# A graph attention layer on one core: gathers that wait for TensorE, and the output made behind the edge loop, in place of output made inside it and gathers that wait for their buffers alone

## The chip, the cores and the metric

One core of a Trainium2 chip runs the kernel. The metric is device time of one execution in microseconds (us). The engines are named as the profile names them: PE is TensorE (PEld its weight loads), DVE VectorE, ACT ScalarE, POOL GpSimd, SP SyncE. GpSimd's indirect DMAs fetch rows of a table by an index in memory ("gathers"); SyncE issues nearly all other transfers.

## What is computed

A graph has N = 12500 nodes with 128 features x, and E = 212500 edges, sorted by destination, with 128 features each, a weight, a source src and a destination dst. Reference, cut to what matters:

```python
h = relu(layernorm(x))
q = (h @ Wq.T + bq)            # 8 heads of 16
k = edge_attr @ Wk.T + bk      # one row per edge
v = (h @ Wv.T + bv)
in_m, out_m, diag_m = sum(q[src]*k), sum(q[dst]*k), sum(q[src]*q[dst])   # per edge and head
score = (seg_softmax(in_m/4, dst) + seg_softmax(out_m/4, dst) + seg_softmax(diag_m/4, dst)) * weight ** lam
g = segment_sum(score * v[dst], dst)
out = x + leaky_relu(g @ Wo.T + bo, 0.1)
```

Since v[dst] is the same for all edges of a destination, it is enough to sum exponentials (den) and weighted exponentials (num) per destination, three kinds by 8 heads each; the score of a node is num / den, and the rest is work per node.

## The kernel before

`ordered_path` holds all of it (a second path in the file is for inputs of another shape and isn't run here).

*First stage* (lines 645 to 920): the nodes are loaded, normalized and turned, q is made and stored as a table in DRAM (`q_table`), and once more as three bf16 terms (`q3_table`). Indices are laid out by blocks. The gathers of the first blocks start here.

*Edge loop* (lines 1233 to 1276). The edges are 416 blocks of 512, taken as S = 5 parts of the sorted list side by side, so that one *turn of t* (T = 84 of them) takes one block of each part: block number g = 5 t + s. A block's work:

- `gather` (621): four indirect DMAs on GpSimd, each 128 rows of `q_table` by src (line 625), into a buffer `qq`. There are QQ = 11 buffers, and turn g issues the gathers of block g + LOOK = g + 9. So they wait until block g - 2 has been read (line 1092 and 1093).
- `fetch_edges` (610): 512 rows of edge features, by SyncE, six blocks ahead.
- `turn` (1061): four PE transposes of the edge features, copied to SBUF by ScalarE as `eT`; `project` (1070): k of the block by PE (a bias matmul, line 1072, and the products, line 1074); `spread_q` (1079): q of the destinations by a matmul with one-hots (line 1083), copied beside the gathered rows by ScalarE (line 1085). `one_hots` (1053) makes the one-hots of the next t on ScalarE.
- `logits` (1087): VectorE multiplies (1092, 1093) and reduces (1095).

Once in five blocks, for the block row t - 1 or t - 2: `turn_logits`, `scan_max`, `powers`, `scan_sums` (VectorE's scans along 512 edges), `turn_sums`, `select`, `to_rows` (matmuls of line 1186, copied by ScalarE to `rows` in line 1191) and `put_rows`, in which SyncE stores five pieces of 42 nodes to DRAM, each part to a table of its own (`sums[s]`).

The order on each engine is the order of the program's calls: `pin` (592) chains an engine's instructions. Turn g of the loop calls, in this order,

```python
gather(g + LOOK); fetch_edges(g + AHEAD)
project(g + 1)
turn(g + 2); spread_q(g + 2)
logits(g)
one_hots(t + 1, s)
# by s: turn_logits, turn_sums | scan_max | to_rows, powers | scan_sums, fetch | select, put_rows
nodes_between(t, s)
```

so PE's *turn g* is k of block g + 1, transposes and one-hot products of block g + 2, and what stands there by s.

*Output.* A unit is 256 nodes; there are 49. The class `Nodes` (935) makes the output of two of them: `load_sums`, `load_x`, `normalize`, `scores`, `turn`, `project_v`, `turn`, `project_o`, `store`. 40 of the 49 units lie in one part only and are done before the last turns; `stored_at` (527) works out from when, and `nodes_between` (1206) makes two of them in each two turns of t, in pieces after the blocks' own work. The other 9 units come behind the loop (1279 to 1298). In the loop's first five turns ScalarE's queue zeroes the five tables of sums (1274).

Of the kernel before, what the change touches and what calls it, by code (L numbers as in the profile page):

```python
# [472 lines left out]
def ordered_path(ctx: ExitStack, tc: tile.TileContext, flag, x, src, dst, edge_attr, edge_weight,  # L473
# [17 lines left out]


# [22 lines left out]
    UN = 2 * P  # L515
    LAST = N // 2 - (NU - 1) * P
    assert NI % 2 == 0 and NU % CU == 0 and N % 2 == 0 and 96 <= LAST < P

    START, RATE, NEAR = round(G * BE * N / E), BE * N // E, 90

    def parts_of(u):

        return [s for s in range(S)
                if (s == 0 or START * s + RATE - NEAR < UN * (u + 1))
                and (s == S - 1 or UN * u < START * (s + 1) + RATE + NEAR)]

    def stored_at(u):

        of = parts_of(u)
        t = -(-(UN * (u + 1) + NEAR - START * of[0]) // RATE)  # L530
        return t + 2 if len(of) == 1 and t < T else None
# [6 lines left out]
    sums = [dram.tile([NP, 2 * H3], F32, name=f"sums{i}") for i in range(S)]  # L538
# [40 lines left out]
    blank = consts.tile([P, 2 * 2 * H3], F32, name="blank")  # L579
# [3 lines left out]
    bases = consts.tile([1, T, S], I32, name="bases")  # L583
    tops = consts.tile([1, T, S], I32, name="tops")
# [23 lines left out]
    qqs, st, eas = {}, {}, {}  # L608
# [12 lines left out]
    def gather(g):  # L621
        if g < S * T:
            qq = gath.tile([P, JN, 2, F], F32, name="qq")
            for j in range(JN):
                pin(nc.gpsimd.indirect_dma_start(  # L625
                    out=qq[:, j, 0, :], out_offset=None, in_=q_table,
                    in_offset=bass.IndirectOffsetOnAxis(
                        ap=src_i[:, g % S * G + g // S, j:j + 1], axis=0)))
            qqs[g] = qq
# [15 lines left out]
    with tc.tile_pool(name="prep", bufs=1) as prep, \  # L645
# [15 lines left out]
        for i, b in enumerate((bv, bk, bo)):  # L661
            pin(nc.sync.dma_start(b_row[:, i, :], b[None, :]))
        due = prep.tile([1, T, S], F32, name="due")
        nc.gpsimd.iota(due, pattern=[[RATE, T], [START, S]], base=0, channel_multiplier=0,
                       allow_small_or_imprecise_dtypes=True)
# [207 lines left out]
        for g in range(-2, GN):  # L873
            if g + 2 < GN:
                rectify(g + 2)
            if 0 <= g + 1 < GN:
                turn_h(g + 1)
            if g >= 0:
                nodes_q(g)
            ready(g + 4)  # L880
            measure(g + 6 + min(max(g, 0), 6))
            if g in side:
                side[g]()
# [10 lines left out]
        found = prep.tile([1, 7], F32, name="found")  # L894
# [4 lines left out]
        base_f = prep.tile([1, T, S], F32, name="base_f", tag="terms")  # L899
# [11 lines left out]
        nc.vector.tensor_reduce(found[:, 3:4], halo[:, 0:S - 2], AX.X, ALU.max)  # L911

        far = top_f
        nc.vector.tensor_sub(far, base_f, due)
        nc.vector.tensor_reduce(found[:, 4:5], far, AX.XY, ALU.min)
        nc.vector.tensor_scalar(found[:, 4:5], found[:, 4:5], -float(NEAR), None, op0=ALU.is_lt)
        nc.vector.tensor_reduce(found[:, 5:6], far[:, 0:2], AX.XY, ALU.max)
        nc.vector.tensor_scalar(found[:, 5:6], found[:, 5:6], float(NEAR), None, op0=ALU.is_gt)
        nc.vector.tensor_reduce(found[:, 6:7], found[:, 0:6], AX.X, ALU.max)
        nc.vector.tensor_copy(flag, found[:, 6:7])  # L920


    fin = ctx.enter_context(tc.tile_pool(name="fin", bufs=2))

    def unit_in(to, u):

        to = to.rearrange("p k f -> p (k f)")
        if u < NU - 1:
            pin(nc.sync.dma_start(to, units(x, u, 1, F)[:, 0, :]))
        else:  # L930
            pin(nc.gpsimd.memset(to[96:, :], 0.0))
            pin(nc.sync.dma_start(to[:LAST, :],
                                  x[u * UN:, :].rearrange("(p k) f -> p (k f)", k=2)))

    class Nodes:

        def __init__(self, of):
            self.of = of  # L940
            self.n = 2 * len(of)

        def load_x(self):
            self.x = fin.tile([P, JN, F], F32, name="x_in", bufs=4)
            for i, u in enumerate(self.of):
                unit_in(self.x[:, 2 * i:2 * i + 2, :], u)

        def load_sums(self):
            self.ab = fin.tile([P, JN, 2 * H3], F32, name="ab", bufs=3)
            for i, u in enumerate(self.of):  # L950
                for j, t in enumerate(parts_of(u)):
                    to = self.ab
                    if j > 0:
                        to = self.more = fin.tile([P, JN, 2 * H3], F32, name="more", bufs=3)
                    pin(nc.sync.dma_start(to[:, 2 * i:2 * i + 2, :].rearrange("p k c -> p (k c)"),
                                          units(sums[t], u, 1, 2 * H3)[:, 0, :]))
                    if j > 0:
                        both = self.ab[:, 2 * i:2 * i + 2, :]
                        pin(nc.vector.tensor_add(both, both, to[:, 2 * i:2 * i + 2, :]))

        def normalize(self, lo, hi):
            if lo == 0:
                self.h = fin.tile([P, JN, F], F32, name="h", bufs=4)
            for b in range(lo, min(hi, self.n)):
                n = 2 * self.of[b // 2] + b % 2
                pin(nc.scalar.activation(self.h[:, b, :], self.x[:, b, :], AF.Relu,
                                         bias=shift[:, n:n + 1], scale=inv[:, n:n + 1]))

        def scores(self):
            n = self.n  # L970
            den, num = self.ab[:, :n, 0:H3], self.ab[:, :n, H3:]
            pin(nc.vector.tensor_scalar(den, den, 1e-30, None, op0=ALU.max))
            pin(nc.vector.reciprocal(den, den))
            pin(nc.vector.tensor_mul(num, num, den))
            score = self.score = fin.tile([P, JN, HEADS], F32, name="score")
            pin(nc.vector.tensor_add(score[:, :n], num[:, :, 0:HEADS], num[:, :, HEADS:2 * HEADS]))
            pin(nc.vector.tensor_add(score[:, :n], score[:, :n], num[:, :, 2 * HEADS:]))

        def turn(self, to):
            for b in range(self.n):  # L980
                pin(nc.tensor.transpose(to[:, b, :], self.h[:, b, :], ident))
            self.hT = fin.tile([P, JN, P], F32, name="hT")
            pin(nc.scalar.copy(self.hT[:, :self.n], to[:, :self.n]))

        def product(self, to, bias, w):
            pin(nc.tensor.matmul(to[:, :self.n, :], ones3, bias[:, :self.n, :], start=True, stop=False))
            for b in range(self.n):
                pin(nc.tensor.matmul(to[:, b, :], self.hT[:, b, :], w, start=False,
                                     stop=(b == self.n - 1)))

        def project_v(self, to):
            self.product(to, bv3, wv)
            pin(nc.vector.tensor_mul(
                self.h[:, :self.n, :].rearrange("p n (h d) -> p (n h) d", d=DIM),
                to[:, :self.n, :].rearrange("p n (h d) -> p (n h) d", d=DIM),
                self.score[:, :self.n, :].rearrange("p n h -> p (n h)")[:, :, None]
                .to_broadcast([P, self.n * HEADS, DIM])))

        def project_o(self, to):
            n = self.n  # L1000
            self.product(to, bo3, wo)
            o, y = self.h[:, :n], self.x[:, :n]
            pin(nc.scalar.copy(o, to[:, :n]))
            pin(nc.vector.scalar_tensor_tensor(o, o, SLOPE, o, op0=ALU.mult, op1=ALU.max))
            pin(nc.vector.tensor_add(y, o, y))  # L1005

        def store(self):
            for i, u in enumerate(self.of):
                y = self.x[:, 2 * i:2 * i + 2, :].rearrange("p k f -> p (k f)")
                if u < NU - 1:  # L1010
                    pin(nc.sync.dma_start(units(out, u, 1, F)[:, 0, :], y))
                else:
                    pin(nc.sync.dma_start(out[u * UN:, :].rearrange("(p k) f -> p (k f)", k=2),
                                          y[:LAST, :]))


    pairs, todo = {}, sorted((stored_at(u), u) for u in range(NU) if stored_at(u) is not None)
    for t in range(0, T - 1, 2):
        if len(todo) > 1 and todo[1][0] <= t:
            pairs[t] = Nodes([todo.pop(0)[1], todo.pop(0)[1]])  # L1020
# [3 lines left out]
    with tc.tile_pool(name="work", bufs=2) as work, \  # L1024
# [181 lines left out]
        def nodes_between(t, s):  # L1206
            new, old = pairs.get(t - t % 2), pairs.get(t - t % 2 - 2)
            even = t % 2 == 0
            if new and even and s == 0:
                new.load_sums()  # L1210
                new.load_x()
# [3 lines left out]
            if new and even and s == 3:  # L1215
                new.normalize(2, 4)
# [127 lines left out]
```

## Time and profile before

| | us |
|---|---|
| three executions, lowest, median, highest | 3223.39, 3225.73, 3229.08 |
| the profiled execution | 3225.73 |
| its span, first to last instruction | 3223.6 |
| first stage, until the first reduction of the loop (line 1095) | 0 to 177.1 |
| edge loop, first to last reduction | 177.1 to 3149.5 |
| last gather's end | 3089.0 |
| behind the last reduction | 3149.5 to 3223.6 |
| gathers (line 625): 1680 | 1013 ns each in the mean, 0.30 between two |
| granted TensorE clock, mean | 0.713 |

The profile's rows are groups of instructions: line, engine, operation, output<-input tile and shape, count, busy time and mean duration of one, then the idle time of that engine just before them and what ended it. A row of the waits names who waited, for whom, the total, the count and the longest. "remote" there is a release whose origin the profile can't name; "issue" is idle time in which nothing that the profile shows was waited for.

### The profile page before, as it was taken

Reading aid. Unit: us, or ns where it says so; the run is one execution under the profiler, and the core shown is the slowest. Engines: PE = TensorE matmul, PEld = TensorE weight load, DVE = VectorE, ACT = ScalarE, POOL = GpSimd, SP = SyncE. Lnnn points to the kernel's source line nnn. Section 1 sums busy time; section 2 is a strip of 40 time slices with the busy share of each in tenths; the row PEclk is TensorE's granted clock in tenths of the full one; section 3 lists DMA queues with packets and bytes.
Section 4 is the critical chain, followed back from the end, with each engine's and each line's share of the span. In section 5 each row is a group of like instructions: output and inputs, shape, how many; then the busy total and the mean of one; then the engine's idle time right before and its main releaser. Section 6 shows DMA issues by size and latency. Waiting matters only on the chain. (4 is left out here: it accounts for less than half of the span.)

```text
span 3223.6 us, 35159 instructions
## 1 busy us (share of the span) xinstructions
PE 1876.1 (58%) x10629; PEld 1492.6 (46%) x10629; DVE 2153.3 (67%) x2263; ACT 1511.4 (47%) x2797; POOL 1736.7 (54%) x1715
## 2 busy tenths in 40 slices
PE   5155555565565665665656566565655665656665
PEld 4134444454444544543545455454544544445453
DVE  7556656666576767766766677576757766766684
ACT  6444434444454444544544454444444544544452
POOL 4645555555555655655555555555655665555520
PEclk8567766666677767776777677667767776777686
DMA  6653333333343334433433433333333433433321
GB/s 188 211 154 96 94 92 98 100 97 93 96 114 100 102 95 108 113 99 98 120 97 96 110 110 104 100 107 103 103 94 109 112 98 99 115 102 96 110 56 44
DMA packets 306675, 340.99 MB, mean 106 GB/s; under 512 B 137667, under 2 KB 225496, under 8 KB 306165
## 3 DMA queue, kind: packets, MB, share of 16 engines
q1 hardware_dynamic: 244906, 222.99, 23.6%
q0 software_dynamic: 54448, 112.96, 14.0%
q10 hardware_dynamic: 7120, 2.70, 0.3%
q8 instruction: 85, 1.39, 0.2%
q14 instruction: 116, 0.95, 0.1%
HBM read 307.79 MB, written 30.64 MB: 105 GB/s over the span
## 5 line engine op out<-in xcount | busy, mean ns | idle before, releaser
L625 POOL DMA_INDIRECT qq<-q_table,src_i x1680 | 1702.0, 1013 | 1304.6 <-ACT qq L1085 517.8
L1074 PE MATMUL k_ps<-wk,eT 128*128 128x128 f32 x3360 | 681.1, 365 | 734.1 <-ACT eT L1066 587.6
L1074 PEld LDWEIGHTS k_ps<-wk,eT 128*128 128x128 f32 x3360 | 579.0, 260 | 965.3 <-ACT eT L1066 685.9
L1095 DVE TENSOR_REDUCE lT<-prod 128x96 f32<-128x1536 f32 x420 | 736.2, 1753 | 14.3
L1093 DVE TENSOR_TENSOR prod<-qq,k_ps 128x1024 f32<-128x1024 f32 x420 | 510.2, 1215 | 135.6 <-remote 108.0
L1066 ACT COPY eT<-eT_ps 128x512 f32<-128x512 f32 x420 | 245.1, 584 | 751.6 <-remote 246.5
L1149 DVE TENSOR_TENSOR ew<-e,att_ps 120x512 f32<-120x512 f32 x84 | 57.8, 688 | 783.6 <-ACT e L1140 771.7
L1064 PE MATMUL eT_ps<-ident,ea 128*128 128x128 f32 x1680 | 350.9, 348 | 4.6 <-DVE found L897 2.9
L1083 PE MATMUL qd_ps<-win,oh 126*128 126x128 bf16 x1680 | 226.5, 261 | 210.7 <-issue 164.4
L1085 ACT COPY qq<-qd_ps 128x512 f32<-128x512 f32 x420 | 247.6, 590 | 176.5 <-PE eT_ps L1064 69.8
L1058 ACT ACTIVATE relb<-relb,before 126x512 bf16<-126x512 bf16 x420 | 307.3, 732 | 7.3 <-DMA relb<-rel_d 7.3
L1092 DVE TENSOR_TENSOR prod<-qq 128x512 f32<-128x512 f32 x420 | 285.8, 680 | 31.4 <-ACT qq L1085 16.9
L1064 PEld LDWEIGHTS eT_ps<-ident,ea 128*128 128x128 f32 x1680 | 282.7, 186 | 4.5 <-DVE found L897 3.2
L1191 ACT COPY rows<-w_ps 126x288 f32<-126x288 f32 x84 | 33.1, 394 | 530.5 <-remote 500.4
L1083 PEld LDWEIGHTS <-oh 126*128 126x128 bf16 x1680 | 172.0, 121 | 220.3 <-issue 174.2
L1059 ACT ACTIVATE oh<-relb 126x512 bf16<-126x512 bf16 x420 | 264.5, 630 | 13.8
L1072 PE MATMUL k_ps<-b,ones 3*128 3x512 bf16 x420 | 196.8, 469 | 105.2 <-issue 81.3
L1186 PE MATMUL w_ps<-back,sel 128*126 128x144 f32 x1344 | 204.2, 301 | 41.6 <-issue 40.9
L1173 PE MATMUL b_ps<-ident,sum 120*128 120x120 f32 x672 | 132.6, 324 | 136.0 <-ACT l L1115 118.1
L1186 PEld LDWEIGHTS w_ps<-back,sel 128*126 128x126 f32 x1344 | 182.4, 198 | 44.2 <-issue 43.2
L1173 PEld LDWEIGHTS b_ps<-ident,sum 120*128 120x128 f32 x672 | 97.2, 213 | 172.4 <-ACT l L1115 131.5
L1174 ACT COPY back<-b_ps 128x480 f32<-128x480 f32 x168 | 97.6, 581 | 45.9 <-PE b_ps L1173 35.0
(170 smaller groups left out, 1782.7 us busy)
## 6 DMA issues: line engine op xcount, KB each, us to landing
ea<-in_edge_attr_dram SPq DMA_DIRECT2D x419, 256.0 KB
relb<-rel_d SPq DMA_DIRECT2D x84, 630.0 KB
qq<-q_table,src_i POOLq DMA_INDIRECT x1680
win<-q_table SPq DMA_DIRECT2D x420, 31.5 KB
q_table<-q SPq DMA_DIRECT2D x24, 384.0 KB
fa<-fa_d SPq DMA_DIRECT2D x420, 4.0 KB
sums<-rows SPq DMA_DIRECT2D x416, 7.9 KB
q_table<-xq SPq DMA_DIRECT2D x24, 256.0 KB
```

The costliest lines, as they stand in the source:

```text
L625: pin(nc.gpsimd.indirect_dma_start(out=qq[:, j, 0, :], out_offset=None, in_=q_table, in_offset=bass.IndirectOffsetOnAxis(ap=src_i[:, g % S ...
L1058: pin(nc.scalar.activation(d, d, AF.Abs, bias=before[:K3]))
L1059: pin(nc.scalar.activation(st[t]["oh"][:, s, :], d, AF.Relu, bias=1.0, scale=-1.0))
L1064: pin(nc.tensor.transpose(eT_ps[:, j, :], eas[g][:, j * F:(j + 1) * F], ident))
L1066: pin(nc.scalar.copy(eT, eT_ps))
L1074: pin(nc.tensor.matmul(k_ps[:, j, :], eTs[g][:, j, :], wk, start=False, stop=(j == JN - 1)))
L1083: pin(nc.tensor.matmul(qd_ps[:, j, :], d["oh"][:, s, j * P:(j + 1) * P], d["win"][:, s, :], start=(j == 0), stop=(j == JN - 1)))
L1085: pin(nc.scalar.copy(qqs[g][:, :, 1, :], qd_ps))
L1092: pin(nc.vector.tensor_mul(prod[:, :, 2, :], qqs[g][:, :, 0, :], qqs[g][:, :, 1, :]))
L1093: pin(nc.vector.tensor_mul(prod[:, :, 0:2, :], qqs[g], ks[g][:, :, None, :].to_broadcast([P, JN, 2, F])))
L1095: pin(nc.vector.tensor_reduce(lTs[t][:, :, s, :], prod.rearrange("p j i (h d) -> p j (i h) d", d=DIM), AX.X, ALU.add))
L1186: pin(nc.tensor.matmul(w_ps[:, i].rearrange("p s c -> p (s c)"), d["sel"][:, j, lo:lo + 3, :].rearrange("p s w -> p (s w)"), d["back"][:, ...
```

## The change

Four parts.

1. *Gates on the gathers.* `gather` gets a dependency with a semaphore: the first gather of block g + 9 waits for the last PE instruction of `project(g)`, which turn g - 1 issues, and the third for the last PE instruction of turn g - 1. The waits for the buffers stay. The second and the fourth follow in GpSimd's order.
2. *The output leaves the loop.* `Nodes`, `nodes_between`, `parts_of`, `stored_at` and a part of the input test go. Behind the loop, after the edge buffers are given back, all 49 units are made in seven chunks of seven.
3. *Two tables of sums in place of five*: part s stores to table s % 2, and the output adds the two. Stores to the same table wait for each other.
4. *The zeros* are stored in the first stage, by SyncE between the stores of q, in place of ScalarE's queue in the first turns of the loop.

The built program shows the gates as waits for PE's semaphore on the first and the third gather of each block, and SyncE's third, fourth and fifth store of sums in a turn with a wait for the store two before. In the last part PE's order has the next group's transposes ahead of a group's last products.

```diff
-    sums = [dram.tile([NP, 2 * H3], F32, name=f"sums{i}") for i in range(S)]
+    sums = [dram.tile([NP, 2 * H3], F32, name=f"sums{i}") for i in range(2)]
...
             for j in range(JN):
-                pin(nc.gpsimd.indirect_dma_start(
+                rows = pin(nc.gpsimd.indirect_dma_start(
                     out=qq[:, j, 0, :], out_offset=None, in_=q_table,
...
+                if (g - LOOK, j) in behind:
+                    tc.add_manual_dep(rows.ins, behind[g - LOOK, j], mybir.DependencyInfo(
+                        mybir.DependencyClass.Sync, mybir.DependencyReason.SCHED_ONLY),
+                        reason="close behind the products")
...
+            if 0 <= g < NI // CU:
+                for t in sums:
+                    pin(nc.sync.dma_start(t.rearrange("(p i) r -> p (i r)", p=P)
+                                          [:, g * CU * 2 * H3:(g + 1) * CU * 2 * H3], blank))
...
-                        pin(nc.sync.dma_start(sums[lo + k][bass.ds(base_v[t][lo + k], W), :],
+                        pin(nc.sync.dma_start(sums[(lo + k) % 2][bass.ds(base_v[t][lo + k], W), :],
                                               st[t]["rows"][k * W:(k + 1) * W, i, k, :]))
...
+        products = str(mybir.EngineType.PE)
...
             if g + 1 < end:
                 project(g + 1)
+                behind[g + 1, 0] = pinned[products]
...
-            nodes_between(t, s)
-            if g < S:
-                of = [u for u in range(NU) if g in parts_of(u)]
-                pin(nc.scalar.dma_start(
-                    units(sums[g], of[0], len(of), 2 * H3),
-                    blank[:, None, :].to_broadcast([P, len(of), 2 * 2 * H3])))
+            behind[g + 1, 2] = pinned[products]
+
+    edges.close()
+    with tc.tile_pool(name="fin", bufs=2) as fin, \
+            tc.tile_pool(name="fin_ps", bufs=2, space=PSUM) as fin_ps:
+        for lo in range(0, NU, CU):
+            ab = fin.tile([P, 2, CH, 2 * H3], F32, name="ab", bufs=3)
+            for i in range(2):
+                nc.sync.dma_start(ab[:, i].rearrange("p (u k) r -> p u (k r)", k=2),
+                                  units(sums[i], lo, CU, 2 * H3))
+            x_in = fin.tile([P, CH, F], F32, name="x_in", bufs=3)
+            nodes_in(x_in, lo, CU, nc.sync)
...
+            for i in range(CH):
+                n = 2 * lo + i
+                nc.scalar.activation(h[:, i, :], x_in[:, i, :], AF.Relu, bias=shift[:, n:n + 1],
+                                     scale=inv[:, n:n + 1])
...
+            for i in range(0, CH, JN):
...
+                for b in range(nb):
+                    nc.tensor.transpose(h_ps[:, b, :], h[:, i + b, :], ident)
...
+                nc.scalar.copy(hT[:, :nb], h_ps[:, :nb])
...
+                nc.tensor.matmul(v_ps[:, :nb, :], ones3, bv3[:, :nb, :], start=True, stop=False)
...
```

The rest of the last part is the work of `Nodes` on groups of four tiles of 128 nodes: products with wv, the score, transposes, products with wo, the leaky rectifier and the sum with x.

## The prediction

> **What bounds the kernel now.** I read five views in this order: the page's busy shares, the turns of the edge loop (start of each first reduction, line 1095), the waits of its middle (800 to 2800 us), one turn in the timeline, and busy time by stretch.
>
> ```profile
> PE 1876.1 (58%) x10629; PEld 1492.6 (46%) x10629; DVE 2153.3 (67%) x2263; ACT 1511.4 (47%) x2797; POOL 1736.7 (54%) x1715
> ```
>
> No engine is full, so some wait bounds the loop. In the trace the loop's first reduction starts at 177.1 us, that of its last turn at 3139.5: 83 turns of 35.7 us in the mean (36.5 over turns 2 to 18, where no output is made, 35.5 after). Yet the last turn, when GpSimd has no gather left (its last ends at 3089), takes 26.4 us. VectorE's rows add up to 24.5 us a turn (5 x (0.68 + 1.215 + 1.753) plus three scans of 1.27, 0.69, 0.69 and 1.02). So about 10 us a turn are lost, and only while there are gathers.
>
> ```profile
> DVE ew L1149 <- ACT e L1140: 489.5, 51, 13.1
> POOL qq L625 <- ACT qq L1085: 309.9, 37, 10.5
> ACT rows L1191 <- remote: 307.2, 35, 12.5
> ```
>
> These are the waits of 800 to 2800 us (total, times, longest). VectorE waits for ScalarE, ScalarE's copy of rows waits for a "remote" (nothing that the profile can name), and GpSimd waits about 10 us at a time. One turn, from the timeline (start, us, engine, line; in brackets the idle time before):
>
> ```profile
> 1605.24 0.95 POOL L625 DMA_INDIRECT qq<-q_table,src_i  x1 [10.34 <-ACT qq L1085]
> ...
> 1615.61 0.60 PE L1064 MATMUL eT_ps<-ident,ea 128*128 128x128 f32 x4
> ...
> 1616.27 2.18 PE L1186 MATMUL w_ps<-back,sel 128*126 128x144 f32 x16
> ...
> 1618.49 0.58 ACT L1066 COPY eT<-eT_ps 128x512 f32<-128x512 f32 x1 [2.16 <-PE w_ps L1186]
> ...
> 1630.69 0.95 POOL L625 DMA_INDIRECT qq<-q_table,src_i  x1 [0.30 <-issue]
> 1634.24 0.40 ACT L1191 COPY rows<-w_ps 126x288 f32<-126x288 f32 x1 [11.03 <-remote]
> ```
>
> The copy of eT needs transposes that ended at 1616.21, but starts at 1618.49; the copy of rows needs matmuls that ended at 1618.45, but starts at 1634.24. TensorE had done its work; its semaphore updates arrived late. The trace's semaphore records show five PE updates at once, 1634.21 to 1634.47. GpSimd meanwhile ran 20 gathers without a break, 1605.24 to 1631.64. It is so everywhere: of the 76 unbroken runs of 16 or more gathers after the start, each is followed by that volley of PE updates 2.35 to 3.00 us (median 2.78) after its last gather ended. Early in a run, updates are prompt; they go late some 10 us into it.
>
> ```profile
> 1605.00:1616.00 11.00, 9.19 (x59) 7.70 (x60) 10.90 (x10) 7.37 (x14) 8.55 (x8) 0.84 0.57 165
> 1616.00:1634.00 18.00, 5.53 (x41) 4.13 (x39) 8.76 (x12) 2.76 (x5) 12.05 (x12) 0.73 0.27 71
> ```
>
> Busy us of PE, PEld, DVE, ACT, POOL, then clock, DMA share, GB/s. In the first 11 us VectorE is full; in the next 18 it and ScalarE run dry while GpSimd goes on, and the DMA engines are at 27%, so bandwidth is not what holds them. **The loop is bound by TensorE's late semaphore updates under long runs of gathers.**
>
> **The gates (the added wait).** Gathers 0 and 1 of block g + 9 now wait for k of block g, gathers 2 and 3 for the last TensorE instruction of turn g - 1; before, only for the slot (products of block g - 2). Behind them on GpSimd stand only later gathers, whose data are used 8 blocks later, so a late gather costs nobody at once. From the trace of the turn above: k of blocks 201 to 204 ends at 1606.0, 1613.1, 1615.8, 1620.3; TensorE's turns 200 to 202 end at 1610.7, 1614.4, 1618.8. A pair takes 2.5 us (0.95 + 0.30 each). So the pairs of blocks 210, 211 and the first of 212 would start at 1606.0, 1610.7, 1613.2, 1615.7 and 1618.2, with a pause of 2.2 us after the first. The second pair of 212 needs the update of 1618.8, which came at 1634.2: GpSimd would stop at 1620.4, ten gathers into the turn instead of twenty, and 2.8 us later the updates would come, at 1623.2 instead of 1634.2. The gate starves on the very update that the gathers hold up, so a run ends itself.
>
> What a turn then costs: 20 gathers without a pause take 26.4 us (a run of 20 lasts 26.1, plus 0.3). One stop of 2.8 us for each run of ten gives 26.2 + 2 x 2.8 = 31.8 us. The other neighbour is a stretch of before in which GpSimd happened to be held back by its slots:
>
> ```profile
> 2564.67 0.94 POOL L625 DMA_INDIRECT qq<-q_table,src_i  x1 [1.05 <-ACT eT L1066]
> ...
> 2571.29 0.95 POOL L625 DMA_INDIRECT qq<-q_table,src_i  x1 [1.05 <-ACT l L1114]
> ...
> 2580.75 0.95 POOL L625 DMA_INDIRECT qq<-q_table,src_i  x1 [0.31 <-issue]
> ```
>
> Here two pauses of 1.05 us stand among 15 gathers (2559.85 to 2580.75, 14 steps of 1.49 us), and TensorE's updates stay prompt until 7 us after the second: 20 such steps are 29.9 us a turn. The wait itself was not in before, so both ends stay: 26.4 (no lateness left) and 36.5 (nothing gained; for a loss see the rivals). I take **30 us**, between the stretch and the sum with stops: 83 x 30 = 2490 us, where before has 2962. Next late then is GpSimd itself (26.4) with VectorE close by (24.5).
>
> The page "SBUF — State Buffer" of the Trainium skill, section "SBUF: two separate sides", says that TensorE and ScalarE never wait on anyone and that only GpSimd and VectorE share a port. By it nothing that GpSimd does could hold TensorE, the gate would gain nothing, and the sum would be the 36.5 us a turn of the first rival; the 11.03 us row above speaks against it here.
>
> **Output taken out of the loop.** 20 pairs of units go: each 3.65 us of VectorE, 3.46 of ScalarE, 5.56 of TensorE (rows of lines 966 to 1005, busy over 16 pairs). Together 73, 69 and 111 us, but the turns with them are no longer than those without (35.5 against 36.5), so I count their removal at nothing. If VectorE became the bound it would give back up to 73 us.
>
> **Output at the end.** All 98 tiles of 128 nodes now come behind the loop: 24.5 groups of four. A group is 5.56 us of TensorE (transposes 1.71, products 2.84, biases 1.01), more than the other two engines; in the built order TensorE takes the next group's transposes between, so that only VectorE's 0.68 us product is partly open. I take 6.2 us: 152 us (136 if all is hidden, 206 at the 8.4 us that a chain with three open copies would take). In front: from the last block's reduction (3149.5) to the last store of sums (3173.5) 24 us as now, some 9 us until they land and the first chunk is read; behind, 5 us for last copy, sums and store. 190 us, against 74.1 now (3149.5 to 3223.6): +116.
>
> **Zeros and sums.** 28 DMAs of 172 KB (4.8 MB) on SyncE's queue among the q stores take the place of 5 DMAs of 528 KB on ScalarE's in turns 0 to 4. The first 177 us move 195 GB/s at a DMA share of 0.65: 4.8 MB are 25 us if they are in the way, 0 if not; I take 10. With two tables of sums instead of five, the third to fifth store of a turn waits for the one two before it to land (a store of 1634.66 landed by 1636.0): some 4 us a turn on SyncE, behind which the edge loads stand. These are needed four blocks later, and SyncE waits for TensorE in nearly every turn (line 1050, up to 17.8 us), so 0; uncovered it would be 4 x 83 = 330 us, inside the range of the gate.
>
> **Sum** against the profiled execution (span 3223.6 us; the execution took 3225.73, which is also the median, 2.1 outside the span): 177.1 + 10 + 2490 + 10.0 (rest of the last turn) + 190 + 2.1 = **2880 us**.
>
> **Rivals.**
> - *No lateness left*: the natural pauses of the gates keep updates prompt, as in the stretch of 2559 us. For it: that stretch, and the 26.4 us of a turn without gathers. Against: 20 gathers need the whole 26.4 us, so pauses must be short. 83 x 26.4 = 2191: **2580 us**. VectorE's load would make it a little more: eight gathers beside a full VectorE took 8.55 us, 1.07 each.
> - *Half gained*: runs still reach ten gathers and the restart is slow (ScalarE has 5 us of work queued after 1634.2). From 34.2 us a turn the change is no gain: **3230 us**, 33 to 35 us giving 3130 to 3300.
> - *The gate does not bind* (slower): if updates get late for another reason, or the wait is always met because GpSimd trails TensorE, the cycle of 36.5 us stays and the output of the end is added. 83 x 36.5 = 3030: **3420 us**. Against it: in the turn above eight of the first ten gathers ran ahead of their gate. It decides from 34.2 us a turn.
> - *Each pair pays the stop* (slower): if the update that the next pair needs comes only 2.8 us after a pair's end, ten pairs cost (2.2 + 2.8 + 0.1) x 10 = 51 us a turn: **4620 us**. Against it: updates are prompt in the first 5 to 10 us of a run.
>
> **Chances.** Forecast 0.60, its own range 28.5 to 32.5 us a turn, 2755 to 3090. No lateness 0.17; half gained 0.05; gate does not bind 0.12; each pair pays 0.06. The range has to take in the second case and most of the third: 2560 (no lateness, the end's output 16 us cheaper) to 3230, which leaves out 0.19. Faster by over 0.2% (about what a measurement of this kernel can tell from no change): 0.60 + 0.17 + 0.02 = 0.79; same 0.02; slower 0.12 + 0.06 + 0.01 = 0.19.
>
> **What will show it.** Right: no GpSimd run of 16 or more gathers, GpSimd's idle time split into many pieces of 1 to 3 us released by TensorE, rows' wait for "remote" gone from the top of the waits, turns near 30 us, an end of about 190 us. Wrong: turns of 36 us, runs of 20, or "remote" waits as long as before; or TensorE's updates late although the runs are short, which would clear the gathers of the blame.

## The result and the profile after

| | us |
|---|---|
| before, median of 4 (lowest, highest) | 3225.86 (3223.39, 3229.08) |
| after, median of 4 (lowest, highest) | 2990.49 (2986.17, 2993.02) |
| ratio after / before, 95% interval | 0.9268 [0.9252, 0.9284] |

The change is faster by 7.3% on this chip. The forecast was 2880, its range 2560 to 3230. The profiled execution took 2987.99 us, its span is 2986.2:

| step | forecast | measured |
|---|---|---|
| until the first reduction of the loop | 187.1 | 184.1 |
| 83 turns | 2490 (30.0 each) | 2606 (31.4 each) |
| last turn, first to last reduction | 10.0 | 18.9 |
| behind the last reduction | 190 | 176.9 |
| outside the span | 2.1 | 1.8 |
| sum | 2880 | 2988 |

The prediction read one time of before wrongly. The first reduction of the last turn starts at 3130.58 us, not at 3139.5, which is its third:

```profile
3130.58 1.75 DVE L1095 TENSOR_REDUCE lT<-prod 128x96 f32<-128x1536 f32 x1
...
3139.53 1.75 DVE L1095 TENSOR_REDUCE lT<-prod 128x96 f32<-128x1536 f32 x1
...
3149.51 1.75 DVE L1095 TENSOR_REDUCE lT<-prod 128x96 f32<-128x1536 f32 x1
```

So the 83 turns of before take 2953.5 us (35.6 each, for 2962 and 35.7), and its last turn 18.9 us from first to last reduction, as in after.

The lines of the source have moved: in after the gathers are line 608, the copy of eT 946, the copy of rows 1071, the reduction 975. First line of the page, then waits of 800 to 2700 us (who waits, for whom, total, times, longest):

```profile
PE 1880.0 (63%) x10635; PEld 1506.6 (50%) x10635; DVE 2162.2 (72%) x2178; ACT 1515.0 (51%) x2806; POOL 1716.4 (57%) x1714
```

```profile
POOL qq L608 <- issue: 282.1, 912, 2.1
...
ACT eT L946 <- remote: 170.1, 50, 7.4
POOL qq L608 <- ACT eT L946: 150.5, 58, 3.0
ACT rows L1071 <- remote: 141.7, 36, 4.4
```

The work is the same (TensorE 1880 us against 1876, VectorE 2162 against 2153); what has gone is idle time. The copy of rows now waits at most 4.4 us for a "remote", where it waited up to 12.5, and GpSimd's waits of 10 us are gone. But the "remote" waits are not gone: those of the copy of eT, 188.8 us in total and up to 8.0 in before, are 170.1 and 7.4 in after. One turn in the timeline shows what became of them:

```profile
1609.40 2.18 PE L1066 MATMUL w_ps<-back,sel 128*126 128x144 f32 x16
...
1612.86 0.94 POOL L608 DMA_INDIRECT qq<-q_table,src_i  x1 [0.30 <-issue]
...
1615.22 0.40 ACT L1071 COPY rows<-w_ps 126x288 f32<-126x288 f32 x1 [3.49 <-PE qd_ps L963]
1615.49 0.94 POOL L608 DMA_INDIRECT qq<-q_table,src_i  x1 [1.69 <-PE qd_ps L963]
...
1627.09 0.94 POOL L608 DMA_INDIRECT qq<-q_table,src_i  x1 [0.31 <-issue]
1630.00 0.59 ACT L946 COPY eT<-eT_ps 128x512 f32<-128x512 f32 x1 [3.24 <-remote]
...
1630.64 0.94 POOL L608 DMA_INDIRECT qq<-q_table,src_i  x1 [2.61 <-ACT eT L946]
```

Read it from the gathers. A run of eight ends at 1613.80 because the next gather's gate is not open. The products of rows ended at 1611.58, yet their copy starts at 1615.22, 1.4 us after the last gather; then GpSimd goes on, and a run of ten ends at 1628.03. This repeats: the runs of after are 82 of eight gathers, 72 of ten and 76 of two, and, in the loop, a single one of 16 (before: 59 of twenty, 21 of sixteen). The loop's gathers stop 243 times for 511 us together, 2.1 us each. Per turn that is 20 x 1.000 of gathers, 17 x 0.307 between them and 6.2 of stops: 31.4 us. The profile names ScalarE's copy of eT or VectorE's scan u (line 1005) for many of the stops. By the times of the semaphore updates, two of the three stops of a turn (1.7 and 2.0 us) end 0.07 and 0.26 us (median) after an update of TensorE; the third (2.6 us) ends 0.05 us after a copy of eT, 0.46 after the last update of a volley.

To compare kernels by one number, I count in the trace's records of TensorE's main semaphore the *bunches*: three or more updates with less than 0.15 us from one to the next, from 400 to 2000 us. In before there are 48, and they come 2.77 us (median) after the last gather of a run; in after 100, 1.53 us after it. The volleys are more, and GpSimd makes room for them sooner; they are not smaller (mostly five updates in before, six or four in after). That it is the updates that are late, and not the matmuls, can be read in the turn of before that the prediction shows: between the first and the last update of the volley of 1634.21 to 1634.47 lie, by their order, the matmuls from 1618.38 to 1623.01, some 3 us of work by their rows, which 0.26 us can't hold. (The Trainium skill, page "Perfetto Trace Analysis", section "Summary: the profiler window per engine type", says that TensorE's end in a profile is an estimate and that the propagation of its semaphore update is hidden from it. This trace agrees: the copy of rows starts 15.8 us after the profiled end of its products.)

Busy time by stretch (PE, PEld, DVE, ACT, POOL, then clock, DMA share, GB/s), loop and output of after:

```profile
184.00:2809.30 2625.30, 1695.10 (x9579) 1364.20 (x9578) 1969.20 (x1757) 1337.37 (x2411) 1639.52 (x1640) 0.72 0.39 110
...
2835.00:2986.00 151.00, 103.73 (x640) 78.72 (x640) 77.31 (x126) 79.78 (x182) 0.31 (x1) 0.87 0.42 118
```

TensorE is the busiest engine of the output behind the loop, as the prediction had it, with 104 of the 151 us.

### The profile page after: what moved, and what is told of

The parts are those of the page before. It is cut to its first block, busy times and chain, and to the rows that moved or that the text cites. A ratio compares the mean times of both kernels' runs of the same rounds, so it can differ in the third digit from the quotient of the medians.

```text
span 2986.2 us, 35917 instructions
## 1 busy us (share of the span) xinstructions
PE 1880.0 (63%) x10635; PEld 1506.6 (50%) x10635; DVE 2162.2 (72%) x2178; ACT 1515.0 (51%) x2806; POOL 1716.4 (57%) x1714
## 4 chain that ended last, share of the span: by engine, by line
PE 36%; ACT 22%; another core or an unknown queue 14%; issue 12%; DVE 5%; DMA 4%; POOL 4%; SPq 1%; POOLq 1%; ACTq 0%; DVEq 0%
PE k_ps L954 14%; PE eT_ps L944 5%; ACT relb L938 4%; POOL qq L608 4%; ACT qq L965 4%; PE b_ps L1053 4%; ACT oh L939 4%; PE qd_ps L963 3%; PE k_ps L952 3%; DMA qq<-q_table,src_i 3%; PE w_ps L1066 2%; ACT l L995 2%; ACT up L1016 1%; ACT down L1017 1%
## 5 line engine op out<-in xcount | busy, mean ns | idle before, releaser
L608 POOL DMA_INDIRECT qq<-q_table,src_i x1680 | 1683.5, 1002 | 991.3 <-issue 396.7
L954 PE MATMUL k_ps<-wk,eT 128*128 128x128 f32 x3360 | 698.9, 372 | 391.6 <-ACT keep L1021 316.3
L954 PEld LDWEIGHTS k_ps<-wk,eT 128*128 128x128 f32 x3360 | 596.0, 267 | 618.6 <-ACT keep L1021 338.2
L1053 PE MATMUL b_ps<-ident,sum 120*128 120x120 f32 x672 | 158.3, 377 | 417.8 <-ACT l L995 377.7
L1053 PEld LDWEIGHTS b_ps<-ident,sum 120*128 120x128 f32 x672 | 108.5, 216 | 461.6 <-ACT l L995 394.5
L963 PE MATMUL qd_ps<-win,oh 126*128 126x128 bf16 x1680 | 210.1, 263 | 92.5 <-issue 42.6
L1066 PE MATMUL w_ps<-back,sel 128*126 128x144 f32 x1344 | 188.5, 295 | 1.3 <-ACT back L1054 1.3
L1066 PEld LDWEIGHTS w_ps<-back,sel 128*126 128x126 f32 x1344 | 174.4, 193 | 2.0 <-ACT back L1054 2.0
L1005 DVE TENSOR_TENSOR_SCAN u<-l,u,far_ps 120x512 f32<-120x512 f32 x83 | 106.2, 1279 | 48.7 <-ACT l L995 44.7
```

Of the source, the lines that this page charges most:

```text
L608: rows = pin(nc.gpsimd.indirect_dma_start(out=qq[:, j, 0, :], out_offset=None, in_=q_table, in_offset=bass.IndirectOffsetOnAxis(ap=src_i[: ...
L954: pin(nc.tensor.matmul(k_ps[:, j, :], eTs[g][:, j, :], wk, start=False, stop=(j == JN - 1)))
L963: pin(nc.tensor.matmul(qd_ps[:, j, :], d["oh"][:, s, j * P:(j + 1) * P], d["win"][:, s, :], start=(j == 0), stop=(j == JN - 1)))
L1053: pin(nc.tensor.transpose(b_ps[:, j, :], d["nd"][i][:, j:BE:JN], ident[:R, :R]))
L1066: pin(nc.tensor.matmul(w_ps[:, i].rearrange("p s c -> p (s c)"), d["sel"][:, j, lo:lo + 3, :].rearrange("p s w -> p (s w)"), d["back"][:, ...
```

## The experiments

Theory: GpSimd's gathers hold up TensorE's updates, and the gates end the runs. Rival A: the gain comes from the output that no longer interrupts the loop. Rival B: any unbroken work of GpSimd holds the updates up. Rival C: it is the bytes of the gathers. "Turn" is the mean of the 83 turns, "bunches" is the count above; "before there" is the kernel before on the same chip. The runs with long fills, a quarter of the bytes, no gathers, half the gathers, and two short fills by block are one execution each.

| run | time | before there | turn | bunches |
|---|---|---|---|---|
| before | 3225.9 | | 35.6 | 48 |
| after | 2990.5 | 3225.9 | 31.4 | 100 |
| after, no gates | 3386.6 | 3217.6 | 36.2 | 44 |
| before, gates | 2838.6 | 3217.6 | 31.0 | 108 |
| after, no gates, long fills | 2908.7 | 3217.6 | 30.3 | 60 |
| after, no gates, quarter bytes | 3191.6 | 3217.6 | 33.8 | 50 |
| after, no gates, no gathers | 2322.1 | 3217.5 | 23.4 | 0 |
| before, four short fills by two blocks | 2863.1 | 3217.5 | 31.3 | 57 |
| before, two short fills by block | 2759.0 | 3217.5 | 30.0 | 15 |
| before, gate of k alone | 2907.3 | 3217.5 | 31.7 | 94 |
| after, no gates, half the gathers | 2322.5 | **2370.4** | 23.4 | 0 |
| before, gates and short fills | 2736.0 | **2370.4** | 29.6 | 0 |
| before, four gates | 2376.7 | **2370.4** | 25.4 | 0 |
| after, four gates | 2931.0 | 3214.5 | 30.7 | 93 |

**The changed kernel without the gates.**

```diff
-                if (g - LOOK, j) in behind:
-                    tc.add_manual_dep(rows.ins, behind[g - LOOK, j], ...
```

> The changed kernel without its gates; all else stays (output behind the loop, two tables, zeros in the first stage). Theory (the gates end the long runs of gathers, and with them the late updates of TensorE): runs of 16 to 20 gathers come back and a turn goes from 31.4 us back to 35.5 to 36.5. 184 + 83 x 35.5 to 36.5 (2947 to 3030) + 10 + 177 + 2 = 3320 to 3403 us, slower than the kernel before. Rival A (the gain is the output that no longer interrupts the loop): turns stay near 31.4 us and the time near 2990 us.

3386.61 us, ratio to before 1.0521 [1.0504, 1.0539]: 79 runs of twenty gathers, turns of 36.5 (median). Rival A falls; without the gates the rest of the change costs time. Its waits (800 to 2700 us) are those of before, and longer:

```profile
DVE ew L1025 <- ACT e L1016: 668.7, 52, 14.2
...
ACT rows L1067 <- remote: 519.7, 52, 13.7
```

**The kernel before with the gates alone.**

```diff
+                if (g - LOOK, j) in behind:
+                    tc.add_manual_dep(rows.ins, behind[g - LOOK, j], ...
...
+                behind[g + 1, 0] = pinned[str(mybir.EngineType.PE)]
...
+            behind[g + 1, 2] = pinned[str(mybir.EngineType.PE)]
```

> The kernel before with the gates alone; the output stays in the loop, with five tables of sums and zeros on ScalarE's queue. Theory: the runs end after some ten gathers and a turn costs about 31.4 us; the output in the loop lies beside it as in the kernel before. 177 + 83 x 31.4 (2606) + 10 + 74 + 2 = 2870 us, bounds 2820 to 2960 (the output's 73 us of VectorE and 111 us of TensorE partly in the way). Rival A: the gates alone do nothing, 3226 us.

2838.62 us, ratio 0.8813 [0.8792, 0.8835]: it beats both kernels. The gates give all of the gain, and the output in the loop costs nothing here (31.0 us a turn against 31.4 without it). The other parts of the change together cost some 150 to 170 us (2990.5 against 2838.6 with gates, 3386.6 against 3217.6 without).

```profile
POOL qq L625 <- issue: 303.5, 948, 2.1
...
ACT eT L1070 <- remote: 115.9, 33, 8.2
```

**Pauses of GpSimd that wait for nothing.** In the changed kernel without gates, with a scratch tile `idle` of 128x2560 f32:

```diff
             qq = gath.tile([P, JN, 2, F], F32, name="qq")
+            if g >= 2 * LOOK and g % 2 == 0:
+                pin(nc.gpsimd.memset(idle["t"], 0.0))
```

> The changed kernel without gates, but GpSimd fills a scratch tile of 128x2560 f32 ahead of the gathers of each second block (from block 18 on), a pause of 2 to 4 us after at most 8 gathers that is tied to no TensorE work. Theory, if it is the gathers that hold the updates up: TensorE's updates get through in the pauses, the 'remote' waits fall to those of the changed kernel, and a turn is GpSimd's own work: 26.4 + 2.5 x (2 to 4) = 31 to 36 us, 2970 to 3390 us in all. Rival B (any unbroken GpSimd work holds the updates up, or only a wait of GpSimd frees them): runs of 20 gathers with fills between, late updates and 'remote' waits as before, and turns of 36.5 + 2.5 x (2 to 4) = 41 to 46 us, 3800 to 4200 us.

2908.68 us, turns of 30.3, with no wait of a gather for TensorE at all from 800 to 2700 us: the theory's side, 61 us under its bounds. It is not what the gate waits for that helps, but that the gathers stop. Rival B falls for fills of this length: GpSimd is at work through the whole pause, and the updates come in it, 1.7 us after the last gather, as in a pause by a gate:

```profile
1605.09 0.94 POOL L610 DMA_INDIRECT qq<-q_table,src_i  x1 [0.30 <-issue]
...
1606.03 2.25 POOL L608 MEMSET idle<- 128x2560 f32 x1
...
1607.72 0.58 ACT L945 COPY eT<-eT_ps 128x512 f32<-128x512 f32 x1 [6.20 <-remote]
```

**Gathers of a quarter of the bytes**, from the twelfth block on, without gates:

```diff
-                    out=qq[:, j, 0, :], out_offset=None, in_=q_table,
+                    out=qq[:, j, 0, :F // 4], out_offset=None,
+                    in_=q_table.rearrange("n (a f) -> (n a) f", a=4),
```

> The changed kernel without gates, with gathers of 128 bytes a row in place of 512 from the eleventh block on (three quarters of each gathered row are left out; the number of gathers and of rows stays). Theory in its first form (what holds the updates up is the making of the gathers' descriptors on GpSimd, as many as before): runs of 16 to 20 gathers, updates late by about 10 us, turns of 35 to 36.5 us, 3320 to 3400 us. Rival C (the bytes in the queue hold them up: a run writes 20 x 64 KB): updates come in time, turns of 26.4 to 30 us, 2570 to 2870 us.

3191.58 us, turns of 32.3 or 36 (mean 33.8): 1.2 us a turn below the theory's bounds, 3.8 above the rival's. The mechanism is there (runs of 16, copies of eT that wait up to 13 us), so Rival C falls as the whole cause; a part of the delay may still go with the bytes. (The index now picks quarters of rows out of the first quarter of the table, so where the reads go has changed too.) Why the runs are of 16 and 4 in place of 20 was not followed.

```profile
ACT eT L945 <- remote: 439.2, 60, 13.0
```

The trace speaks against the transfer from another side. Taking the packets of the gathers' queue in order, 32 to a gather, the data of a gather in the kernel without gates land 1.18 to 1.22 us (median) after its instruction ended, at each place of a run from the sixth on: the queue shows no backlog there while ScalarE waits up to 13.7 us for an update. Half of the 32 packets are of 4 bytes; with a quarter of the bytes their number, and that of all packets, is the same. Whether the delay goes with the number of gathers or of packets is not shown by any run here.

**No gathers** from the twelfth block on, without gates: `for j in range(JN) if g < QQ else ():`, and block g reads the rows of block g % 11.

> The changed kernel without gates and without gathers from the twelfth block on (the rows gathered for the first eleven blocks are read again; so the gathered q of all later blocks is left out). Theory: no update of TensorE is late for long, no wait for 'remote' above 2 us in the loop, and a turn is 24.5 us (VectorE's rows) to 27 us (the last turn of the kernel before took 26.4): 184 + 83 x 24.5 to 27 + 10 + 177 + 2 = 2407 to 2614 us. Rival (late updates have another cause, such as SyncE's transfers): turns of 30 us or more, above 2860 us.

2322.05 us: 23.4 us a turn, no bunch, and no wait for "remote" at all from 400 to 2100 us. This is the theory's side, 85 us under its bounds. On this chip the kernel before took 3217.5. Against the 36.2 us a turn of the same kernel with its gathers, on another chip with the same time of before, the gathers cost some 13 us a turn.

```profile
PE 1700.0 (73%) x10635; PEld 1367.2 (59%) x10635; DVE 2132.5 (92%) x2178; ACT 1494.5 (64%) x2806; POOL 80.8 (3%) x78
```

VectorE is at 92%: this is what the loop is worth without gathers when nothing is late. It is also below the 24.5 us that the prediction added up for VectorE's rows: in the trace the durations add up to 24.4 us a turn, but each row starts a little before the last one's end, and the engine is busy for 23.2.

**Short fills**, in the kernel before, without gates: four of 128x256 f32 ahead of the gathers of each second block, or two ahead of those of every block (2 in place of 4, and no `g % 2 == 0`).

```diff
+            for _ in range(4 if g >= 2 * LOOK and g % 2 == 0 else 0):
+                pin(nc.gpsimd.memset(idle["t"], 0.0))
```

> The kernel before (no gates, output in the loop) with four fills of 128x256 f32 on GpSimd ahead of the gathers of each second block: a pause of some 1.2 us after each eight gathers. If such a pause is enough for the updates to pass: a turn is GpSimd's work, 20 x 1.28 + 2.5 x 1.2 = 28.7 us, 177 + 83 x 28.7 + 96 = 2655 us (2600 to 2720). If it is too short (in the run with fills of 2.25 us the updates came 1.7 us after the last gather): the runs of gathers count on through the pause, updates stay late, and turns are 31 to 39 us, 2850 to 3500 us.

2863.13 us, ratio 0.888 [0.885, 0.891], turns of 31.3: the low end of the second forecast. From one gather's end to the next's start the pause is 1.85 us (2.41 with the long fill). Most bunches (53 of 57) fall into such pauses, 1.48 us (median) after the last gather, but not all that is late comes through: copies of eT still wait up to 6.9 us for a "remote" (800 to 2500 us), and turns range from 23.4 to 44.4 us.

> The same total of fills, spread: two fills of 128x256 f32 ahead of the gathers of every block, a pause of some 0.6 us after each four gathers. If what holds the updates up drains in proportion to the pauses: as with four fills each second block, 2600 to 2720 us. If a pause has to have a least length: updates late again, turns of 31 to 39 us, 2850 to 3500 us.

2759.04 us (one run), between the two forecasts. The median turn of 28.4 is about what GpSimd's work alone makes (5 x 5.8 us), but 30 of 83 turns are over 32 us, the longest is 48. In the one ahead of that, of 40 us:

```profile
1409.09 0.40 ACT L1194 COPY rows<-w_ps 126x288 f32<-126x288 f32 x1 [3.36 <-remote]
...
1415.64 0.59 ACT L1069 COPY eT<-eT_ps 128x512 f32<-128x512 f32 x1 [4.10 <-remote]
...
1426.55 0.69 DVE L995 TENSOR_TENSOR h<-node_ps,score 128x512 f32<-128x512 f32 x1 [7.96 <-remote]
```

From block 18 on no run is longer than four gathers (4.7 us), and still waits for late updates go on for over 20 us. So the length of one run alone doesn't set it. That lateness builds up over many runs, where the gathers take 4.7 of each 5.8 us, fits this, but isn't shown.

**The gate of k alone**, in the kernel before (the gate on the third gather left out).

> The kernel before with the gate of k alone (first gather of a block); the third gather waits for nothing of TensorE. Theory (a run ends itself when the update that its gate needs is late, whichever it is): the k gate starves as well, runs of 8 to 12 gathers, turns of 31 to 32.5 us, 2840 to 2960 us. Rival (the gate at the turn's end, which is the later one, does the work): runs of 16 to 20 come back, turns of 34 to 36.5 us, 3090 to 3300 us.

2907.25 us, ratio 0.9047 [0.9025, 0.9069]: inside the theory's bounds. The runs are mostly of eight (127) and of four (some 50), with some 35 of 11 to 20; this gate starves too, but less surely, and the second gate is worth 69 us (2839 with both, on another chip with the same time of before).

**Half the gathers; gates and fills; four gates.** These three ran on one chip.

```diff
-            for j in range(JN):
+            for j in range(JN) if g < QQ else range(0, JN, 2):
```

> The changed kernel without gates, with only the first and the third gather of each block from the twelfth block on (half of the gathered q is left out; the rows of the first eleven blocks stand in its place). Without gathers a turn took 23.4 us; with all of them and no gates 36.5. Theory (it is the length of an unbroken run that makes updates late, some ten gathers being the point): ten gathers a turn, runs of at most 10, little lateness, turns of 23.4 to 26.4 us, 2320 to 2570 us. Rival (the cost grows in proportion to the number of gathers, 13.1 us for 20): 23.4 + 6.5 = 30 us a turn, 2860 us.

Two gates and two short fills by block, in the kernel before:

> The kernel before with the gates and with two fills of 128x256 f32 ahead of the gathers of every block (0.7 us after each four gathers). If the fills keep updates prompt in most turns and the gates end the others early: turns of 28.4 (the median with fills alone) to 30 us, 177 + 83 x 28.4 to 30 + 92 = 2626 to 2759 us, below both parts alone (2839 and 2759). If the stops of both add: 31 + 5 x 0.7 = 34.5 us a turn, 3130 us.

A gate on each gather, in the kernel before:

```diff
                 turn(g + 2)
+                behind[g + 1, 1] = pinned[str(mybir.EngineType.PE)]
                 spread_q(g + 2)
+                behind[g + 1, 2] = pinned[str(mybir.EngineType.PE)]
...
-            behind[g + 1, 2] = pinned[str(mybir.EngineType.PE)]
+            behind[g + 1, 3] = pinned[str(mybir.EngineType.PE)]
```

> The kernel before with a gate on each gather: the first of block g + 9 waits for k of block g, the second for the transposes of turn g - 1, the third for its one-hot products, the fourth for the turn's end. If finer gates stop a run earlier and at less backlog: turns of 28 to 30.5 us, 2593 to 2800 us. If the last gate of a turn does all the work, as with two gates: 31 us, 2839 us within 1.5%. If every wait pays the lateness: above 33 us, over 3010 us.

2322.54, 2736.03 and 2376.67 us. None of them tells what it was made for (the first two lie inside the first forecast, but by luck), because on this chip **the kernel before itself takes 2370.35 us** (ten runs, 2368.72 to 2377.76), 26% less than on the others. The program is the same. The four gates there are no gain, 1.0021 [1.0009, 1.0033], and gates with fills are a loss, 1.1554 [1.1529, 1.158]: the fills lengthen GpSimd's work, and turns are 29.6 us. There is no profile of before itself on this chip; that of the kernel with four gates tells why: no bunch and no wait for "remote" is in it, nor in the other two. Its first line, its largest wait of ScalarE (800 to 2200 us), and a stretch of the timeline:

```profile
PE 1724.7 (73%) x10629; PEld 1388.3 (58%) x10629; DVE 2146.6 (90%) x2263; ACT 1491.1 (63%) x2797; POOL 1699.9 (72%) x1715
```

```profile
ACT eT L1070 <- PE eT_ps L1068: 449.9, 190, 5.7
```

```profile
1614.10 1.06 PE L1068 MATMUL eT_ps<-ident,ea 128*128 128x128 f32 x4
...
1615.20 0.59 ACT L1070 COPY eT<-eT_ps 128x512 f32<-128x512 f32 x1 [2.56 <-PE eT_ps L1068]
1615.66 1.09 POOL L625 DMA_INDIRECT qq<-q_table,src_i  x1 [0.30 <-PE qd_ps L1087]
...
1618.42 0.60 PE L1068 MATMUL eT_ps<-ident,ea 128*128 128x128 f32 x4
1619.05 0.58 ACT L1070 COPY eT<-eT_ps 128x512 f32<-128x512 f32 x1 [1.03 <-PE eT_ps L1068]
```

GpSimd runs 1640 gathers in one unbroken row with 0.30 us between them, and these copies of eT start 0.03 and 0.04 us after their transposes. Nothing is late, so the gates stop nothing, and a turn is GpSimd's 20 x 1.29 = 25.8 us (25.4 measured, with the blocks ahead as cushion). The gather takes as long as elsewhere (0.99 us). The clock of 0.815 is no cause: the kernel without gathers had 0.823 on a chip where before takes 3217.5. All runs on this chip are from one session, so whether the chip itself differs or its state at the time is not shown.

**The changed kernel with four gates.**

> The changed kernel with a gate on each gather (k, transposes, one-hot products, turn's end) in place of each second. The last runs were on a chip where no update of TensorE is late and the kernel before takes 2370 us; the others on chips where it takes 3217 to 3226. So two cases. Where the kernel before takes 2370: gates stop nothing, a turn is 25.4 us as in the kernel before with four gates, and the output behind the loop is added in full: 184 + 83 x 25.4 (2108) + 19 + 177 + 2 = 2490 us, 5% slower than before; that would show that the change costs time where updates are prompt. If instead the output in the loop took VectorE's time there, up to 73 us less: 2415 us. Where it takes about 3220: if finer gates stop a run earlier and at less backlog, turns of 28 to 30.5 us, 184 + 2324 to 2532 + 189 = 2697 to 2905 us; if the last gate of a turn does the work, 31.4 us and 2990 us as with two gates; if every wait pays the lateness, above 33 us, over 3110 us.

It ran on a chip where before takes 3214.53: 2930.99 us, ratio 0.911 [0.9093, 0.9127], turns of 30.7. That lies between the forecasts for finer gates (2905 at most) and for no gain by them (2990): they are worth 1.6 points against the two gates of the changed kernel (0.9268, on another chip). The other case, the changed kernel on the chip where nothing is late, was not tried. By the expectation's sum it would take 2490 us there against 2370; that is an estimate from other kernels' rows.

## Why the prediction was right, and where it was off

- *What bounds the loop*: right in four of the five sets of runs. Taking the gates away brings 36.5 us a turn back, taking the gathers away gives 23.4. What the prediction could not see is that the bound does not belong to the program alone: on one chip, in the one session there, the same gathers delay nothing.
- *The gates*: the mechanism was right, the size off. A run does end itself, at eight or ten gathers. The forecast of 30 us stood between "the sum with stops" (31.8) and the paced stretch (29.9); the sum was right (31.4), and the stretch, in which GpSimd was held back by its slots, was no model. The stops are 3 a turn of 2.1 us, 6.2 us, where the prediction had two of 2.8, 5.6 us. 83 x 1.4 = 116 us is more than the whole miss of 108; the last turn adds 9, and the output and the zeros take 16 off.
- *"Early in a run, updates are prompt; they go late some 10 us into it"*: as a rule this fell. With two short fills by block, updates are late at runs of four as well; the length of one run alone doesn't set it.
- *The output out of the loop, counted at nothing*: right here (31.0 against 31.4).
- *The output at the end*: 176.9 for 190. From the first transpose (2844.3) to the last sum (2978.8) it is 134.5 us, 5.5 a group where 6.2 were taken (152); what stands in front is 35 us for 33, what stands behind 7 for 5. TensorE's work was 4.2 us a group (103.7 by 24.5) for 5.56, so it isn't full; that the time came out at "136 if all is hidden" is luck in part.
- *Zeros*: +7.0 for +10. *Five to two tables*: no run tries them alone. The turns of the changed kernel without gates are 36.2 us against 35.6 in before (median 36.5 in both), and which part of the change the difference belongs to is not shown. *Rest of the last turn*: 18.9 us for 10. The 10.0 was measured from the third reduction of that turn; from the first it is 18.9 in before too, and 18.9 without gathers.
- *Rivals*: "the gate does not bind" gave 3420 us from turns of 36.5; the kernel without gates took 3386.6 at those turns, so that price was right. "Each pair pays the stop" needed 51 us a turn; nothing like it was seen, with a gate on each gather either (30.7).
- *The rule of the Trainium skill* that the prediction weighed (page "SBUF — State Buffer", section "SBUF: two separate sides": TensorE never waits on anyone) is about contention for ports of SBUF, and no run here contradicts it: TensorE's matmuls ran on, and it was their updates that came late. What fell on the chips where before takes 3214 us and more is the prediction's inference from it, that nothing GpSimd does could matter; on the one with 2370 a gate on each gather gained nothing (1.0021).

What stays open: why TensorE's updates are held up by gathers, and why not on one chip. The runs above speak against the bytes as the main cause (one execution), a backlog of the gathers' queue, and GpSimd's being busy as such (fills of 2.25 us). Whether the number of gathers or of their packets sets the delay is untested where updates are late, since the run with half the gathers fell on the other chip.

## What to carry to other kernels

If an engine waits for a "remote" long after its producer's last instruction has ended, suspect a late semaphore update: look for the bunch of updates, and for what stopped just before it. A throttle on the source (here a wait, or any other work between the gathers) can be worth more than the work it delays, but measure the parts of a change one by one: here the gates alone gave 0.881, the whole change 0.927. And run both kernels on more than one chip before a workaround is kept: gates gain 12% here and nothing where nothing is late, and gates with fixed pauses lose 15% there.

## What the runs showed of the hardware that was not expected

- The same program took 3214 to 3226 us (medians) on several chips and 2370 on one, each steady within 0.4% over 4 to 10 executions.
- On the slower ones, GpSimd's indirect gathers (0.95 us each, 0.30 between) delay TensorE's semaphore updates, by 15.8 us for the products of rows in the turn of before that the prediction shows, while the gathers' own data land in 1.2 us. With a quarter of the bytes waits of 13 us remain.
- The updates come through 1.5 us after the last gather where runs are of eight to ten, and 2.8 us after it where they are of twenty; also while GpSimd fills memory (1.6 us after the last gather, in a fill of 2.25 us for 128x2560 f32). Pauses of 1.1 us after four gathers (two fills, 0.7 us) are enough for some turns and not for others.
